# First mixture of experts: stationary down weights, rows turned by VectorE, results gathered by token

## The chip, the cores and the metric

The kernel runs on one core of a Trainium2 chip. A core has TensorE (PE, with its weight loads shown as PEld), VectorE (DVE), ScalarE (ACT), GpSimd (POOL) and SyncE (SP), and 16 DMA engines between its on-chip memory (SBUF, 128 partitions) and DRAM. Products of PE land in PSUM, eight banks of 2 KB per partition. The metric is the device time of one execution in microseconds (us); the median of several runs counts.

## The reference

All data are float32. `x` is a table of 1250 nodes by 1024 features; `src` and `dst` are 20,000 edges.

```python
xn = layernorm(x)
x = x + relu(GCNConv(xn, edges)) + linear_attention0(xn)
x = x + moe0(layernorm(x))                  # 8 experts, top 2, at most 391 rows each
xn = layernorm(x)
x = x + SAGE_two_layers(xn, edges) + linear_attention1(xn)
x = x + moe1(layernorm(x))                  # 8 experts, top 2
```

The change is in `moe0`, the first mixture of experts, and in the norm that follows it:

```python
probs = softmax(x @ router_gate)            # 1250 x 8
topw, topi = top_k(probs, 2); topw /= sum(topw)
top_g, tok_idx = top_k(gates.T, 391)        # the 391 rows with the largest gates, per expert
xe = x[tok_idx]                             # 8 x 391 x 1024
h  = silu(xe @ gate_w) * (xe @ up_w)        # hidden width 512
ye = (h @ down_w) * top_g                   # 8 x 391 x 1024
out = zeros(1250, 1024).at[tok_idx].add(ye)
```

So each expert takes up to 391 rows of 1024, multiplies them by two 1024 x 512 matrices and one 512 x 1024 matrix, and the weighted results are added back to the rows that they came from. A row has at most two results.

## The kernel before, in words

The program is a long sequence of stages, each bounded by PE: gather of the edges into a dense adjacency table, the first norm with projections and attention, the graph convolution, routing, the first experts, the second norm with the second attention, the SAGE layers, and the second experts. The whole network stands twice in the program; the second copy runs only for edge lists that need it (`tc.If(many == 1)`), and not in these runs. Rows lie in 10 tiles of 128 (the last has 98). A tile framework gives each operation to its engine's queue in an order that a scheduler decides; on one engine the instructions run in that order, and a waiting instruction holds up those behind it. DMAs are issued from queues too: SP's for most loads, ACT's for some stores, POOL's for indirect ones (gathers and scatters by an index). Pools hand out buffers: a tile of a pool with `bufs=2` waits until the last but one with its name is no longer used. `wpool` has three buffers of 2 MB for all weights. A float32 matmul is two instructions in the trace.

The stages around the change:

**Routing** (L551 to L734). For each tile the norm `normalise` (L587) writes the rows to a DRAM table `x1n_d`; logits, the two experts of each row with their weights `wts`, and the rank of each row within its expert (`above`, L703) follow. The rows of an expert are put in 392 slots, in 4 groups of `GS` = 98. A product of 0/1 matrices (`at_slot` L714, `hit` L717, `what` L719, the matmul `ptab` L726) makes a table with a token index (`idx`) and a gate for each slot. A slot that stays empty points at a spare row behind the 1250.

**First experts** (L738 to L783). The loop runs over 8 experts. For each: four indirect gathers of 98 rows (`xe`, L744, POOL's queue); 32 transposes on PE (`pte`, L750) that turn the rows to `xeT` (features on partitions), evacuated by ACT and DVE in turns (`evac`, L110 and L112); the loads of `wg`, `wu` (L119) and `wd` (L757) on SP's queue; for each of four blocks of 128 hidden features, 8 matmuls each for gate and up (L764), with the weights stationary and 392 columns of `xeT` moving; the Silu on ACT (L766) and the product `hT` on DVE (L767). The down product (L774) has `hT` stationary, 98 columns of it, and `wd` moving, 512 columns; 4 groups x 2 halves x 4 blocks. DVE (L779) and ACT (L777) multiply by the gate to `ye`, and an indirect DMA (L780) adds the rows to the residual `res_d[1]` in DRAM.

**The second norm and the value product** (L789 to L829). POOL clears `proj` and `kv` (L791, L795); SP loads `proj`, `bqT`, `bkT`, biases and the rows. For each of 10 tiles: load `xt` (L825), statistics and norm in place (`layernorm`, L127: BN statistics L130, aggregate L132, square root on ACT L134, reciprocal L136, norm L137), 8 transposes on PE (L145) evacuated to `x1T` by ACT and DVE, 8 matmuls of 512 columns for the value product `pv` (L152) and an addition of the bias (`v`, L829). The keys `pqT` (L807) follow, then a second half of the value columns with weights of its own.

Of the kernel before, what the change touches and what calls it, by code (L numbers as in the profile page):

```python
# [10 lines left out]
F32 = mybir.dt.float32  # L11
# [3 lines left out]
I32 = mybir.dt.int32  # L15
# [27 lines left out]
GS = 98  # L43
NG = SLOTS // GS
# [10 lines left out]
def tile_gps(ctx: ExitStack, tc: tile.TileContext, a: dict, out: bass.AP):  # L55
# [17 lines left out]
    e.ones = const.tile([P, P], F32, name="ones")  # L73
    nc.vector.memset(e.ones, 1.0)
    e.ones_r = const.tile([P, P], F32R, name="ones_r")
    nc.vector.tensor_copy(e.ones_r, e.ones)
# [5 lines left out]
    e.x1n_d = dram.tile([N + GS, D], F32, name="x1n_d")  # L82
# [3 lines left out]

    e.res_d = [dram.tile([N + GS, D], F32, name=f"res{i}_d") for i in range(4)]

# [8 lines left out]
def network(tc: tile.TileContext, a: dict, out: bass.AP, env: SimpleNamespace, exact: bool):  # L97
# [29 lines left out]
    def layernorm(dst, x, ts):  # L127
        st = small.tile([P, 2, 6], F32, name="st")
        for j in range(2):
            nc.vector.bn_stats(st[:ts, j, :], x[:, j * 512:(j + 1) * 512])  # L130
        mv = small.tile([P, 2], F32, name="mv")
        nc.vector.bn_aggr(mv[:ts], st[:ts].rearrange("p a b -> p (a b)"))  # L132
        sd = small.tile([P, 1], F32, name="sd")
        nc.scalar.activation(sd[:ts], mv[:ts, 1:2], AF.Sqrt, bias=eps_t[:ts])  # L134
        rs = small.tile([P, 1], F32, name="rs")
        nc.vector.reciprocal(rs[:ts], sd[:ts])  # L136
        nc.vector.tensor_scalar(dst, x, mv[:ts, 0:1], rs[:ts], op0=OP.subtract, op1=OP.mult)  # L137
# [414 lines left out]
    idx = rp.tile([GS, E * NG], I32, name="idx")  # L552
    gate = rp.tile([GS, E * NG], F32, name="gate")
    with tc.tile_pool(name="route0a", bufs=1) as ra, tc.tile_pool(name="route0w", bufs=2) as rw:
        zero = ra.tile([GS, P], F32, name="zero")
        nc.gpsimd.memset(zero, 0.0)
        for rows in (x1n_d[N:N + GS, :], env.res_d[1][N:N + GS, :]):
            nc.sync.dma_start(rows.rearrange("p (r c) -> p r c", c=P), zero.unsqueeze(1).to_broadcast([GS, KB, P]))
# [3 lines left out]
        trash = ra.tile([P, 1], F32, name="trash")  # L562
        nc.gpsimd.iota(trash, pattern=[[0, 1]], base=N + 1, channel_multiplier=1, allow_small_or_imprecise_dtypes=True)
        slots = ra.tile([P, GS], F32, name="slots")
        nc.gpsimd.iota(slots, pattern=[[1, GS]], base=0, channel_multiplier=0, allow_small_or_imprecise_dtypes=True)
# [8 lines left out]
        wts = ra.tile([P, T, 2], F32, name="wts")  # L574
# [127 lines left out]

        above = ra.tile([P, T, 2], F32, name="above")  # L703
# [4 lines left out]
        nc.vector.tensor_scalar(grp, above, GS - 0.5, None, op0=OP.is_gt)  # L708
        for j in range(2, NG):
            nc.vector.scalar_tensor_tensor(grp, above, j * GS - 0.5, grp, op0=OP.is_gt, op1=OP.add)  # L710
        nc.vector.scalar_tensor_tensor(above, grp, -float(GS), above, op0=OP.mult, op1=OP.add)
        nc.vector.scalar_tensor_tensor(grp, expert, float(NG), grp, op0=OP.mult, op1=OP.add)
        nc.vector.scalar_tensor_tensor(grp, keep, 1000.0, grp, op0=OP.mult, op1=OP.add)
        at = tb.tile([P, T, 2, GS], F32, name="at_slot")  # L714
        nc.vector.tensor_tensor(at, slots.unsqueeze(1).unsqueeze(1).to_broadcast([P, T, 2, GS]),
                                above.unsqueeze(3).to_broadcast([P, T, 2, GS]), op=OP.is_equal)
# [3 lines left out]
        what = tb.tile([P, T, 2, 2, E * NG], F32, name="what")  # L720
        nc.vector.tensor_mul(what[:, :, :, 0], hit, token.unsqueeze(3).to_broadcast([P, T, 2, E * NG]))
        nc.vector.tensor_mul(what[:, :, :, 1], hit, wts.unsqueeze(3).to_broadcast([P, T, 2, E * NG]))
        pt = bank("ptab")
        for t in range(T):
            for k in range(2):
                nc.tensor.matmul(pt[:GS, :2 * E * NG], at[:TS[t], t, k, :],  # L726
                                 what[:TS[t], t, k].rearrange("p a g -> p (a g)"),
                                 start=(t == 0 and k == 0), stop=(t == T - 1 and k == 1))
        nc.scalar.copy(gate, pt[:GS, E * NG:2 * E * NG])
        row = ra.tile([GS, E * NG], F32, name="row")  # L730
        nc.vector.tensor_scalar(row, pt[:GS, :E * NG], 0.5, trash[:GS], op0=OP.is_lt, op1=OP.mult)
        nc.vector.scalar_tensor_tensor(row, pt[:GS, :E * NG], -1.0, row, op0=OP.add, op1=OP.add)
        nc.vector.tensor_copy(idx, row)
# [3 lines left out]

    with s_route:  # L738
        with tc.tile_pool(name="moe0", bufs=2) as mp:
            for e in range(E):  # L740
                xeT = mp.tile([P, KB, SLOTS], F32, name="xeT")
                for g in range(NG):
                    xe = mp.tile([GS, D], F32, name="xe", bufs=4)
                    nc.gpsimd.indirect_dma_start(  # L744
                        out=xe, out_offset=None, in_=x1n_d,
                        in_offset=bass.IndirectOffsetOnAxis(ap=idx[:, e * NG + g:e * NG + g + 1], axis=0))
                    for b0 in (0, 4):
                        pt = bank("pte")
                        for b in range(4):
                            nc.tensor.transpose(pt[:, b * GS:(b + 1) * GS], xe[:, (b0 + b) * P:(b0 + b + 1) * P],  # L750
                                                ident[:GS, :GS])
                        evac(xeT[:, b0:b0 + 4, g * GS:(g + 1) * GS],
                             pt[:, :4 * GS].rearrange("p (b q) -> p b q", b=4))
                wg = load_w(a["L0_ffn_gate_w"][e], 0, "wg")
                wu = load_w(a["L0_ffn_up_w"][e], 0, "wu")
                wd = wpool.tile([P, I0 // P, D], F32, name="wd", tag="w")
                nc.sync.dma_start(wd, a["L0_ffn_down_w"][e].rearrange("(k p) f -> p k f", p=P))  # L757
                hT = mp.tile([P, I0 // P, SLOTS], F32, name="hT")
                for i in range(I0 // P):
                    ic = slice(i * P, (i + 1) * P)  # L760
                    pg, pu = bank("pgate"), bank("pup")
                    for pw, w in ((pg, wg), (pu, wu)):
                        for k in range(KB):
                            nc.tensor.matmul(pw[:, :SLOTS], w[:, k, ic], xeT[:, k, :], start=(k == 0), stop=(k == KB - 1))  # L764
                    sg = mp.tile([P, SLOTS], F32, name="sg")
                    nc.scalar.activation(sg, pg[:, :SLOTS], AF.Silu)  # L766
                    nc.vector.tensor_mul(hT[:, i, :], sg, pu[:, :SLOTS])  # L767
                for g in range(NG):
                    ye = mp.tile([GS, D], F32, name="ye", bufs=3)
                    own = gate[:, e * NG + g:e * NG + g + 1]  # L770
                    for half in range(2):
                        py = bank("py")
                        for i in range(I0 // P):
                            nc.tensor.matmul(py[:GS], hT[:, i, g * GS:(g + 1) * GS], wd[:, i, half * 512:(half + 1) * 512],  # L774
                                             start=(i == 0), stop=(i == I0 // P - 1))
                        if half:
                            nc.scalar.activation(ye[:, 512:], py[:GS], AF.Copy, scale=own)  # L777
                        else:
                            nc.vector.tensor_scalar(ye[:, :512], py[:GS], own, None, op0=OP.mult)  # L779
                    nc.gpsimd.indirect_dma_start(  # L780
                        out=env.res_d[1], out_offset=bass.IndirectOffsetOnAxis(
                            ap=idx[:, e * NG + g:e * NG + g + 1], axis=0),
                        in_=ye, in_offset=None, compute_op=OP.add)  # L783
# [5 lines left out]
    with tc.tile_pool(name="mix1", bufs=1) as mp:  # L789
# [23 lines left out]
        with tc.tile_pool(name="mix1k", bufs=2) as kp:  # L813
            for half in range(2):
                wv = load_w(a["L1_mix_Wv"], half * 512, "wv1")
                bv = bcast(kp, a["L1_mix_bv"], half * 512, 512, "bv1", bufs=1)
                wk = load_w(a["L1_mix_Wk"], half * 512, "wk1")
                v = kp.tile([P, T, 512], F32, name="v1", bufs=1)
# [3 lines left out]
                for t in range(T):  # L822
                    if half == 0:
                        xt = lnp.tile([P, D], F32, name="xt2")
                        nc.sync.dma_start(xt[:TS[t]], env.res_d[1][TOK[t], :])  # L825
                        layernorm(xt[:TS[t]], xt[:TS[t]], TS[t])
                        transpose_rows(xT, xt[:TS[t]], t, KB)
                    pv = rows_of(xT, t, wv, "pv1")
                    nc.vector.tensor_add(v[:TS[t], t, :], pv[:TS[t]], bv[:TS[t]])  # L829
                s_ln.close()  # L830
                for pair in range(4):
                    hp = half * 4 + pair
                    kT = heads_T(kp, wk, bkT, half, pair)
                    kf = kp.tile([P, T, P], F32, name="kf1")
# [14 lines left out]
                    for j in range(2):  # L849
                        nc.vector.tensor_copy(kv[j * 64:(j + 1) * 64, hp, j * 64:(j + 1) * 64],  # L850
                                              pkv[j * 64:(j + 1) * 64, j * 64:(j + 1) * 64])
        with tc.tile_pool(name="attn1T", bufs=1) as ap_:
# [415 lines left out]
```

## Time and profile before

| what | value |
| --- | --- |
| runs | 3616.58, 3617.64, 3618.37 us; median 3617.64 |
| profiled execution | 3615.68 us; its span, first to last instruction: 3613.9 us |
| mean granted PE clock | 0.971 of full speed |
| PE busy | 3447.9 us (95%), 12658 instructions |
| PEld (weight loads, beside PE) | 2064.1 us (57%) |
| DVE busy | 846.4 us (23%), 2356 instructions |
| ACT busy | 315.8 us (9%) |
| POOL busy | 546.5 us (15%) |
| DMA | 326.25 MB, mean 90 GB/s |
| chain that ended last | PE 90%, DVE 4%, DMA 2%, waiting for issue 2% |

A row of a group names the line, the engine, the operation, output and inputs by the program's names, the shape and the count; then busy time in us and the mean of one in ns, and the idle time before it with what ended it. The mean of one matmul is its latency; matmuls are pipelined, so the time that one adds is a stretch divided by its count. A row of the chain gives start, duration, engine, and what it worked on. A row of the table by stretch gives, for one stretch of time, the busy us (and count) of PE, PEld, DVE, ACT and POOL, the granted clock, the share of DMA and the GB/s moved.

### The profile page before, as it was taken

Reading aid. Unit: us, or ns where it says so; the run is one execution under the profiler, and the core shown is the slowest. Engines: PE = TensorE matmul, PEld = TensorE weight load, DVE = VectorE, ACT = ScalarE, POOL = GpSimd, SP = SyncE. Lnnn points to the kernel's source line nnn. Section 1 sums busy time; section 2 is a strip of 40 time slices with the busy share of each in tenths; the row PEclk is TensorE's granted clock in tenths of the full one; section 3 lists DMA queues with packets and bytes.
Section 4 is the critical chain, followed back from the end, with each engine's and each line's share of the span. In section 5 each row is a group of like instructions: output and inputs, shape, how many; then the busy total and the mean of one; then the engine's idle time right before and its main releaser. Section 6 shows DMA issues by size and latency. Waiting matters only on the chain.

```text
span 3613.9 us, 30826 instructions
## 1 busy us (share of the span) xinstructions
PE 3447.9 (95%) x12658; PEld 2064.1 (57%) x12658; DVE 846.4 (23%) x2356; ACT 315.8 (9%) x640; POOL 546.5 (15%) x442
## 2 busy tenths in 40 slices
PE   7999999999997799999979999999999999988997
PEld 3474756644655554555435465546777555556775
DVE  4256344521226301100130000001111111241111
ACT  1000011100001000100011011100000000001111
POOL 0016774051000011111100000010000000003221
PEclk9999999999997699999989999999999999998999
DMA  4725221162232144544430010131000010228884
GB/s 147 167 69 108 24 24 1 46 223 71 74 105 71 36 132 134 144 117 123 123 97 27 24 47 24 44 103 43 24 24 24 35 58 28 79 81 275 278 257 99
DMA packets 165824, 326.25 MB, mean 90 GB/s; under 512 B 36590, under 2 KB 46261, under 8 KB 165545
## 3 DMA queue, kind: packets, MB, share of 16 engines
q1 hardware_dynamic: 114984, 242.08, 20.1%
q0 software_dynamic: 40016, 54.11, 8.7%
q10 hardware_dynamic: 10672, 27.99, 2.2%
q8 instruction: 102, 1.67, 0.2%
q14 instruction: 50, 0.40, 0.0%
HBM read 250.37 MB, written 73.76 MB: 90 GB/s over the span
## 4 chain that ended last, share of the span: by engine, by line
PE 90%; DVE 4%; DMA 2%; issue 2%; ACT 1%; POOL 0%; SPq 0%; ACTq 0%; POOLq 0%; DVEq 0%
PE ph L152 8%; PE ppn L152 8%; PE pwo L152 8%; PE pv L152 8%; PE pqT L807 7%; PE py L774 6%; PE pqk L152 5%; PE p L1198 5%; PE pa L491 5%; PE pgate L764 5%; PE pup L764 5%; PE ph L929 4%; PE py L1209 2%; PE pg L491 2%; PE pkv L345 2%; PE po L393 2%
## 5 line engine op out<-in xcount | busy, mean ns | idle before, releaser
L253 POOL DMA_INDIRECT adj_d<-cnt,cell x167 | 260.0, 1557 | 92.3 <-issue 42.6
L774 PE MATMUL py<-wd,hT 128*98 128x512 f32 x512 | 221.0, 592 | 0.0
L1198 PE MATMUL p<-xeT,w 128*128 128x256 f32 (+1 forms) x1088 | 192.7, 338 | 5.0 <-ACT xeT L110 5.0
L1198 PEld LDWEIGHTS p<-xeT,w 128*128 128x128 f32 x1088 | 171.3, 191 | 25.1 <-ACT xeT L110 9.0
L764 PE MATMUL pgate<-xeT,wg 128*128 128x392 f32 x512 | 175.9, 497 | 1.7 <-ACT xeT L110 1.7
L764 PE MATMUL pup<-xeT,wu 128*128 128x392 f32 x512 | 173.8, 492 | 0.0
L176 POOL TENSOR_TENSOR xr<-xr,bo 128x512 f32<-128x512 f32 (+1 forms) x40 | 50.4, 1264 | 770.4 <-DMA xr<-res_d 601.4
L774 PEld LDWEIGHTS py<-wd,hT 128*98 128x98 f32 x512 | 84.5, 165 | 133.5 <-issue 132.3
L152 PE MATMUL pqk<-wk,x0T 128*128 128x512 f32 (+1 forms) x320 | 145.2, 608 | 9.0 <-ACT x0T L110 7.6
L152 PE MATMUL pv<-wv,x1T 128*128 128x512 f32 (+1 forms) x320 | 141.8, 601 | 2.2 <-ACT x1T L110 2.2
L152 PE MATMUL ph<-ws,h1T 128*128 128x512 f32 (+1 forms) x320 | 143.2, 596 | 0.0
L152 PE MATMUL pqk<-wq,x0T 128*128 128x512 f32 (+1 forms) x320 | 140.7, 593 | 0.0
L764 PEld LDWEIGHTS pgate<-xeT,wg 128*128 128x128 f32 x512 | 97.3, 191 | 72.9 <-ACT xeT L110 3.2
L152 PE MATMUL ppn<-wn,x1T 128*128 128x256 f32 (+1 forms) x640 | 138.8, 379 | 0.0
L929 PE MATMUL ph<-x1T,ws 128*128 128x416 f32 (+1 forms) x384 | 138.2, 512 | 0.0
L152 PE MATMUL pv<-wv,x0T 128*128 128x512 f32 (+1 forms) x320 | 138.0, 592 | 0.0
L152 PE MATMUL ph<-wgcn,x0T 128*128 128x512 f32 (+1 forms) x320 | 138.0, 593 | 0.0
L764 PEld LDWEIGHTS pup<-xeT,wu 128*128 128x128 f32 x512 | 97.3, 190 | 71.3
L152 PE MATMUL pwo<-wo,attn0T 128*128 128x512 f32 (+1 forms) x320 | 137.7, 592 | 0.2 <-ACT attn0T L410 0.2
L152 PE MATMUL ppn<-wn,h1T 128*128 128x512 f32 (+1 forms) x320 | 137.7, 592 | 0.0
L152 PE MATMUL pwo<-wo,attn1T 128*128 128x512 f32 (+1 forms) x320 | 137.5, 592 | 0.0
L807 PE MATMUL pqT<-x1T,wk 128*128 128x416 f32 (+1 forms) x384 | 135.6, 512 | 0.0
(356 smaller groups left out, 4409.3 us busy)
## 6 DMA issues: line engine op xcount, KB each, us to landing
w<-in_L_ffn_w_dram SPq DMA_DIRECT2D x17, 2048.0 KB
w<-in_L_ffn_w_dram SPq DMA_DIRECT2D x17, 1024.0 KB
wg<-in_L_ffn_gate_w_dram SPq DMA_DIRECT2D x8, 2048.0 KB
wu<-in_L_ffn_up_w_dram SPq DMA_DIRECT2D x8, 2048.0 KB
wd<-in_L_ffn_down_w_dram SPq DMA_DIRECT2D x8, 2048.0 KB
adj_d<-ezero SPq DMA_DIRECT2D x2, 6105.0 KB
res_d<-xr SPq DMA_DIRECT2D x45, 256.0 KB
table<-adj_d ACTq DMA_DIRECT2D x36, 312.5 KB
```

Source lines behind the costliest of these rows:

```text
L152: nc.tensor.matmul(pr[:TS[t], :cols], xT[:, k, TOK[t]], w[:, k, :], start=(k == 0), stop=(k == nk - 1))
L176: nc.gpsimd.tensor_add(xr[:TS[t]], xr[:TS[t]], bias[:TS[t]])
L253: nc.gpsimd.indirect_dma_start(out=adj_d[e % 2], out_offset=bass.IndirectOffsetOnAxis(ap=cell[:, e:e + 1], axis=0), in_=cnt[:, e:e + 1], i ...
L345: nc.tensor.matmul(pkv[f][:, :65], kf[:TS[t], i, f * P:(f + 1) * P], v[:TS[t], t, h, :], start=(t == 0), stop=(t == T - 1))
L393: nc.tensor.matmul(po[:TS[t], i, :], qf[:, hh, f, i * P:i * P + TS[t]], kv[:, h, f, :], start=(f == 0), stop=(f == 1))
L491: nc.tensor.matmul(pa, edges if by_node else feats, feats if by_node else edges, start=(s == 0 and i == 0), stop=(s == T - 1 and i == len( ...
L764: nc.tensor.matmul(pw[:, :SLOTS], w[:, k, ic], xeT[:, k, :], start=(k == 0), stop=(k == KB - 1))
L774: nc.tensor.matmul(py[:GS], hT[:, i, g * GS:(g + 1) * GS], wd[:, i, half * 512:(half + 1) * 512], start=(i == 0), stop=(i == I0 // P - 1))
L807: nc.tensor.matmul(pq[:, :n], w[:, k, pair * P:(pair + 1) * P], xT[:, k, c0:c0 + n], start=(k == 0), stop=(k == KB - 1))
L929: nc.tensor.matmul(ps[:, :n], w[:, k, q0 + f * P:q0 + (f + 1) * P], xT[:, k, c0:c0 + n], start=(k == 0), stop=(k == KB - 1))
L1198: nc.tensor.matmul(pw_[:, :n], w12[:, k, off + i * P:off + (i + 1) * P], xeT[:, k, :n], start=(k == 0), stop=(k == KB - 1))
L1209: nc.tensor.matmul(py, hT[:, i, c * P:(c + 1) * P], w3[:, i, half * 512:(half + 1) * 512], start=(i == 0), stop=(i == H1 // P - 1))
```

## The change

Six things change together.

1. **Down product.** `wd` is stationary: for `b` in 0 to 7 the columns `b`, `b+8`, `b+16`, ... (128 of them, 8 apart), and `hT` moves, 392 columns. The result has features on partitions; DVE turns it in blocks of 32 x 32 to `ye` (slots on partitions), after a clear of the 24 columns by which PSUM's 392 are padded to 416.
2. **Rows turned by DVE.** For experts 1 to 7 POOL gathers quarter rows (1 KB each, 128 of them in one DMA, 13 DMAs an expert) into `xq`, laid so that transposes of 32 x 32 blocks on DVE, four an expert, make `xeT`. The gathers and transposes of expert e + 1 are written in the middle of expert e. The first expert keeps gathers of whole rows, 4 of 128 with two buffers, and transposes on PE. `xeT` holds features in the order p x 8 + k, so `wg` and `wu` are loaded with 8 neighbouring rows in each partition.
3. **Slots.** Groups have 128 slots in place of 98. The table product loses the gates and is float32r in place of float32; a second small product (`pspread`) spreads the index table over quarters (`idx_q`).
4. **Results by token.** Each expert's rows are written, not weighted, to a new DRAM table `y_d` by four DMAs. The scatter-add to the residual goes. In the loop of the second norm each tile gathers its two result rows by `slot_of` (POOL), adds them with the weights `wts` on DVE, and writes the sum to `res_d[1]` from ACT's queue, before the norm overwrites the rows in place.
5. **Order.** The gathers and additions of a tile are issued after the norm of the tile before (`issue_after` sets an order, no wait). The weights of the second half are issued after the last tile's row load. A Sqrt on ACT is placed ahead of the norms.
6. **Small ones.** The ones come from the identity; the spare rows are one each; the key pools move.

```diff
 # routing
-        at = tb.tile([P, T, 2, GS], F32, name="at_slot")
+        at = tb.tile([P, T, 2, P], F32R, name="at_slot")
...
-                nc.tensor.matmul(pt[:GS, :2 * E * NG], at[:TS[t], t, k, :],
-                                 what[:TS[t], t, k].rearrange("p a g -> p (a g)"),
+                nc.tensor.matmul(pt[:, :E * NG], at[:TS[t], t, k, :], what[:TS[t], t, k],
                                  start=(t == 0 and k == 0), stop=(t == T - 1 and k == 1))
-        nc.scalar.copy(gate, pt[:GS, E * NG:2 * E * NG])
...
+        pt = bank("pspread")
+        for i in range(4):
+            nc.tensor.matmul(pt[:, i * E * NG:(i + 1) * E * NG], spread_r[:, i, :], row, start=True, stop=True)
...
+        nc.vector.tensor_copy(idx_q, four)
...
+        nc.vector.tensor_copy(env.slot_of, above)
 # first experts
+            def columns(e):
+                xeT = mp.tile([P, KB, ROWS], F32, name="xeT")
+                if e == 0:
+                    for g in range(NG):
+                        n = min(P, SLOTS - g * P)
+                        xe = mp.tile([P, D], F32, name="xe", bufs=2)
+                        nc.gpsimd.indirect_dma_start(
+                            out=xe, out_offset=None, in_=x1n_d,
+                            in_offset=bass.IndirectOffsetOnAxis(ap=idx[:, g:g + 1], axis=0))
+                        for b0 in (0, 4):
+                            pt = bank("pte")
+                            for b in range(4):
+                                nc.tensor.transpose(pt[:, b * P:b * P + n], xe[:n, b0 + b::KB], ident[:n, :n])
+                            evac(xeT[:, b0:b0 + 4, g * P:g * P + n], pt.rearrange("p (b q) -> p b q", b=4)[:, :, :n])
+                else:
+                    xq = mp.tile([P, NI, B, KB], F32, name="xq")
+                    for i in range(NI):
+                        g = e * NG + i // 4
+                        nc.gpsimd.indirect_dma_start(
+                            out=xq[:, i].rearrange("p c b -> p (c b)"), out_offset=None, in_=quarters,
+                            in_offset=bass.IndirectOffsetOnAxis(ap=idx_q[:, i % 4, g:g + 1], axis=0))
+                    for i0 in range(0, NI, 4):
+                        i1 = min(i0 + 4, NI)
+                        nc.vector.transpose(xeT.rearrange("p b (i r) -> p i b r", r=B)[:, i0:i1],
+                                            xq[:, i0:i1].rearrange("p i c b -> p i b c"))
+                return xeT
...
+                    nc.sync.dma_start(w, a[f"L0_ffn_{name}_w"][e].rearrange("(p k) f -> p k f", k=KB))
...
+                    if i == 1 and e + 1 < E:
+                        coming = columns(e + 1)
+                xeT = coming
+                ye = mp.tile([P, NI, B, KB], F32, name="ye")
+                for b in range(KB):
+                    py = bank("py")
+                    for i in range(I0 // P):
+                        nc.tensor.matmul(py[:, :SLOTS], wd[:, i, b::KB], hT[:, i, :],
+                                         start=(i == 0), stop=(i == I0 // P - 1))
+                    nc.vector.memset(py[:, SLOTS:ROWS], 0.0)
+                    nc.vector.transpose(ye[:, :, :, b], py[:, :ROWS].rearrange("p (i r) -> p i r", r=B))
+                for j in range(4):
+                    (nc.sync if e == E - 1 and j % 2 else nc.scalar).dma_start(
+                        env.y_d[e * ROWS:(e + 1) * ROWS, j * KB * B:(j + 1) * KB * B].rearrange("(i r) f -> r i f", r=B),
+                        ye[j * B:(j + 1) * B].rearrange("p i c b -> p i (c b)"))
+    root = small.tile([P, 1], F32, name="root")
+    tc.keep_in_program_order(nc.scalar.activation(root, eps_t, AF.Sqrt))
 # second norm
+                with ExitStack() as s_after:
+                    if half:
+                        s_after.enter_context(tc.issue_after(last_rows.ins))
+                    wv = load_w(a["L1_mix_Wv"], half * 512, "wv1")
...
-                        nc.sync.dma_start(xt[:TS[t]], env.res_d[1][TOK[t], :])
-                        layernorm(xt[:TS[t]], xt[:TS[t]], TS[t])
-                        transpose_rows(xT, xt[:TS[t]], t, KB)
+                        last_rows = nc.sync.dma_start(xt[:ts], env.res_d[1][TOK[t], :])
+                        s_y = ExitStack()
+                        if t:
+                            s_y.enter_context(tc.issue_after(last_norm.ins))
+                        for k in range(2):
+                            yt = lnp.tile([P, D], F32, name=f"yt{k}", bufs=2)
+                            nc.gpsimd.indirect_dma_start(
+                                out=yt[:ts], out_offset=None, in_=env.y_d,
+                                in_offset=bass.IndirectOffsetOnAxis(ap=env.slot_of[:ts, t, k:k + 1], axis=0))
+                            nc.vector.scalar_tensor_tensor(xt[:ts], yt[:ts], env.wts[:ts, t, k:k + 1], xt[:ts],
+                                                           op0=OP.mult, op1=OP.add)
+                        s_y.close()
+                        nc.scalar.dma_start(env.res_d[1][TOK[t], :], xt[:ts])
+                        last_norm = layernorm(xt[:ts], xt[:ts], ts)
+                        transpose_rows(xT, xt[:ts], t, KB)
```

## The prediction, made before the change was run

> **What bounds the kernel now.** First the page: PE is busy 95% of the span and PE makes 90% of the chain that ended last, so time is gained only where PE's own work shrinks or where PE stands still. Then the chain in order of time (start, us, what), for the stages that the change touches:
>
> ```profile
> 1226.98 6.64 DMA xe<-x1n_d,idx
> 1235.23 6.79 PE pgate L764 x16
> ...
> 1278.89 27.47 PE py L774 x64
> 1309.29 5.53 PE pgate L764 x16
> 1314.83 5.27 PE pup L764 x16
> ...
> 1382.09 5.54 PE pgate L764 x16
> ...
> 1788.50 27.48 PE py L774 x64
> 1817.04 8.89 DMA res_d<-ye,idx
> 1829.99 5.99 DMA xt<-res_d
> 1842.30 8.60 PE pv L152 x16
> ...
> 1924.90 16.79 PE pqT L807 x48
> ```
>
> One expert lasts 1382.09 - 1309.29 = 72.8 us: 8 groups of 5.27 (gate and up, 42.1), 27.47 of the down product, and 3.2 left for the 32 transposes of the next rows and their evacuation. The experts run back to back; the last down product ends at 1815.97, and PE then stands still for 26.3 us, until 1842.30. Ten tiles of norm, transposes and value product follow until 1924.90, 82.6 us, 8.25 a tile (1852.01, 1860.26, 1868.51 in the same chain).
>
> Next the table by stretch, for the expert stage (PE, PEld, DVE, ACT, POOL busy, clock, DMA share, GB/s):
>
> ```profile
> 1235.00:1816.00 581.00, 579.30 (x1762) 298.69 (x1760) 58.49 (x93) 50.77 (x93) 71.70 (x56) 1.00 0.45 123
> ```
>
> PE is full, DVE is a tenth busy, DMA not half: room for work taken off PE. Last, rows that price the new operations, from the groups, the timeline and the DMA view of 108 to 148 us (1.6 KB rows written to DRAM):
>
> ```profile
> L774 PE MATMUL py<-wd,hT 128*98 128x512 f32 x512 | 221.0, 592 | 0.0
> L764 PE MATMUL pup<-xeT,wu 128*128 128x392 f32 x512 | 173.8, 492 | 0.0
> L767 DVE TENSOR_TENSOR hT<-sg,pup 128x392 f32<-128x392 f32 x32 | 18.0, 563 | 324.6 <-PE pup L764 324.6
> L540 DVE SCALAR_TENSOR_TENSOR xrg<-rgcn,xrg 128x512 f32<-128x512 f32 (+1 forms) x10 | 6.9, 692 | 0.3
> ```
> ```profile
> 3305.40 7.22 PEld L1198 LDWEIGHTS p<-xeT,w 128*128 128x128 f32 x64 [0.62 <-ACT xeT L110]
> ```
> ```profile
> DMA packets 5632, 9.01 MB, mean 225 GB/s; under 512 B 32, under 2 KB 5630, under 8 KB 5630
> ```
>
> **1. The down product, weights stationary.** It was 64 instructions a expert (each float32 matmul is two) of 512 columns with 98 of 128 weight columns used: 27.47/64 = 0.429 us each. It becomes 8 x 4 matmuls, again 64 instructions, of 392 columns, as in gate and up: 5.27/16 = 0.329. 64 x 0.329 = 21.1; 6.4 saved, x8 = 51.3 us, all on PE's path.
>
> The weights are now read at every eighth column, 32 bytes apart; no stationary operand before is read so. The Trainium skill, "SBUF — State Buffer", section "Door 1: The DMA port swizzle", speaks against this: a line is 16 bytes, and each access that crosses into a new one "pays a penalty", of no stated size. The row: 64 contiguous loads follow each other in 7.22 us, 0.113 each, under matmuls of 128 columns; the new matmuls last 0.329. By the row alone the loads are covered; by the rule, a load two or two and a half times as long is covered still, and costs begin at 2.9 times. I take nothing, with 0 to +120 us (5 times) as the ends, leaning to 0 because 0.113 leaves almost three loads of room.
>
> **2. The row transposes leave PE.** For experts 1 to 7 the 3.2 us a expert go: 7 x 3.2 = 22.2 us. DVE does them as 3.25 transposes of 1024 elements and 8 of 416 from PSUM. No DVE transpose is in the trace; the nearest rows, 392 elements in 0.563 and 512 in 0.692 (1960 in 2.19, at_slot), give about 1.04 ns an element plus 0.16: 1.22 and 0.59 us. In the built order DVE does the four hT products, two row transposes, a memset, the third, the first ye, the fourth, and then memset and ye in turn. At these prices that is some 11 us within the 21 of the down product. The cover: the next rows are due when it ends. Even at four times the price the row transposes and the first ye take 17 us of 21; no gain is excluded below that, and the ends are 0 and +10. I take 0. The ye copies with the gates (0.75 DVE, 0.69 ACT) go too, off the path.
>
> POOL issues 13 gathers of quarter rows a expert, at 1.28 us pitch (0.97 busy, 0.30 gap, as xe has it): 17 of 63 us, where 8 gathers and scatters were; a whole expert ahead, so nobody waits. The gate weights may load from 5.27 + 21.1 = 26.4 us before they are needed (35.6 before); gate and up together, 4 MB, took 15 us after 1273.65, so they stay hidden. ye is stored by four DMAs on ACT's queue, 1.4 us of issue, done before the next Silu, 5.3 us later.
>
> **3. The first expert.** The table product has half the columns and becomes one float32r instruction each: 20 x 0.173 instead of 6.92, -3.5; one product (0.82) less, at_slot +0.63, small ones +0.36, a copy -0.2: index 3.5 earlier. But xe has two buffers, and in POOL's order five gathers of expert 1 stand before the third xe: third issue at 7 x 1.28 = 9.0 after the first instead of 2.6. The first gather was usable 4.5 us after issue (1223.09 to 1227.62), the next each 1.85 later for 98 rows, 2.4 for 128; third at 13.5, fourth at 15.6, transposes 1.3, evacuation 0.5: 17.4 where 1235.15 - 1223.09 = 12.1 were. +5.4 - 3.5: **+2 us**, ends -2 and +6.
>
> **4. From the last product to the value product**, after 1815.97. Memset and ye 1.1; 1.7 MB to y_d in 1 KB rows at the 225 GB/s of the 1.6 KB rows, 7.6, with 1.2 around it: 9.9. POOL's two memsets (0.95 + 1.09) wait for the pool's memory and stand before the gathers: 12. SP sends bqT, bkT, proj and bv before xt, as before (3 us), so xt goes at 12.7 beside yt0 and yt1; sharing the engines, xt lands at 18, yt1 at 20.5. Two additions of 1.22 (692 for 512): 21.8. The sum is stored before the norm overwrites it in place: norm written at 27.4, transposes on a PE slowed by idling (1.94 before) and evacuation: 30. Before 26.3: **+3.7 us**, ends -2 and +10.
>
> **5. The ten tiles.** New on DVE: two additions, 2.45 us a tile, and the wait of the norm (in place) for the store of the sum. The last x3n_d store (0.4 MB) moved its data from 0.7 to 2.5 us after issue; 0.5 MB alone would be 3.2, beside the next tile's gathers I take 4.6 (ends 3.2 and 8). Statistics, Sqrt and reciprocal (2.2) lie under it. Queued behind that wait on DVE are x1T's copy and the next tile's additions; PE waits for the copy, which the built order puts behind the next norm. A tile on DVE: 2.45 + 0.1 + 4.6 + 0.81 (norm) + 0.68 (copy) = 8.65, about 8.8 with the gaps, where PE needs 8.25. The norm of tile 9 then ends at 27.4 + 9 x 8.8 = 106.6; copy and bias 1.4, half of pv 3.5, transposes and evacuation 1.75, last pv 7.1: 120.3, so 90.3 after pv began, 82.6 before: **+7.7 us**, ends 0 and +27 (11 us a tile). Per tile 2 MB in 8.8 us is 238 GB/s; the late experts moved 281 with DMA 0.92 busy, so it fits, barely. The later weights (half 1) have 170 us until needed: nothing.
>
> Sum: -51.3 - 22.2 + 2 + 3.7 + 7.7 = -60.1 us. The profiled execution took 3615.68 (span 3613.9), 2 us under the median of the runs, 3617.64; the difference is carried over: **3557.5 us**.
>
> **Rivals.** (a) The tiles stay with PE (the store lands within 3.5 us, DVE under 8.25 a tile): part 5 is 0 and part 4 about +1, 3547. For it: DVE was only 31 of 83 us busy there. Against: the DVE chain is serial. 0.17. (b) Transfers bind the tiles: gathers at 217 GB/s, load and store share the engines, 12 us a tile: +36 instead of +7.7, 3586. For it: DMA 0.92 busy at 281. 0.13. (c) Slower: in the down product the strided weight loads outlast the matmuls. It decides from 0.329, and the whole gain is gone at 0.329 + 60/512 = 0.446 us, 3.9 times the row's 0.113; at five times, 0.565, the kernel takes 512 x 0.236 = 121 more, 3678. 0.04. (d) The change doesn't free PE: DVE transposes over five us each make PE wait for the rows, 20 us an expert back, about 3610. 0.02. The forecast itself: 0.64.
>
> **How the numbers follow.** 3543 holds (a) with a few us to spare, 3586 takes in most of (b); outside lie (c), (d) and the rest of (b), under 0.2. Runs of before lie 1.8 us apart; 0.2% (7 us) is about what a measurement of this kernel can tell from no change. Faster 0.95; same 0.02, from (d); slower 0.03, the worse part of (c).
>
> **What would show it.** Expert period 63.2 us, py in 21.1, no pte between experts; PEld on py under 0.33 apart; DVE transposes near 1.2 and 0.6 and all of them over before the next pgate; pv beginning 30 us after the last py; tiles 8.8 apart, with DVE's norm waiting for the DMA of res_d. Wrong if the period is over 66 us, or the tiles are over 11 apart.

## The result, and the profile after

The changed kernel takes 3581.14 us (median of 4 runs, 3578.65 to 3586.95) against 3617.32 (4 runs): a ratio of 0.9902, interval 0.9885 to 0.9919, 36 us less. The forecast was 3557.5, range 3543 to 3586. The sign and the range hold; 24 of the 60 us of gain that were forecast are missing.

First the chain that ended last, in order of time, for the stages that the change touches (start, us, engine and what):

```profile
1229.16 6.30 DMA xe<-x1n_d,idx
...
1236.56 7.84 PE pgate L809 x16
...
1249.67 3.29 PE pgate L809 x10
1252.96 1.44 issue
1254.39 0.49 PE pgate L809
1254.88 1.61 issue
1256.49 0.49 PE pgate L809
1256.98 2.32 issue
...
1303.41 21.07 PE py L821 x64
1324.48 5.27 PE pgate L809 x16
...
1387.68 5.27 PE pgate L809 x16
...
1745.81 21.08 PE py L821 x64
...
1768.55 9.42 DMA y_d<-ye
...
1781.76 9.53 DMA yt<-y_d,slot_of
...
1792.83 5.30 DMA res_d<-xt
...
1826.27 2.69 DMA res_d<-xt
...
1848.13 4.29 DMA res_d<-xt
...
1857.30 7.30 DMA res_d<-xt
...
1889.63 16.79 PE pqT L855 x48
```

The first value product is not in this chain; PE's timeline has it:

```profile
1800.91 8.91 PE L158 MATMUL pv<-wv,x1T 128*128 128x512 f32 x16
```

The expert period is 1387.68 - 1324.48 = 63.2 us, the down product 21.07: both as forecast. But the first expert is not like the others: from its first gate product (1236.56) to its down product (1303.41) go 66.9 us, where 42.1 is PE's own work and the kernel before took 1278.89 - 1235.23 = 43.7. In between the chain is made of pieces of "issue": PE waits for nothing that the profile shows. The text calls this the standstill. The ledger, in us, against the kernel before:

| stretch | before | after | difference | forecast |
| --- | --- | --- | --- | --- |
| up to the first gate product | 1235.23 | 1236.56 | +1.3 | +2 |
| first expert up to its down product | 43.7 | 66.9 | **+23.2** | 0 |
| the rest of the experts, to the last down product | 537.1 | 463.5 | -73.6 | -73.5 |
| last down product to the value product | 26.3 | 34.0 | +7.7 | +3.7 |
| value product to the keys | 82.6 | 88.7 | +6.1 | +7.7 |
| after the keys | | | -0.4 | 0 |

The sum is -35.7, and the profiled executions are 3579.93 and 3615.68, -35.75. The forecast is met to 4 us in each stretch but one.

What the standstill looks like: the table by stretch (stretch, its length; busy us and count of PE, PEld, DVE, ACT, POOL; granted clock, DMA share, GB/s), and the longest waits between 1236 and 1282 (who waited for what: us in total, times, longest us; "remote" and "issue" name no engine):

```profile
1250.00:1278.00 28.00, 10.82 (x20) 4.49 (x20) 0.00 (x0) 0.50 (x1) 17.40 (x19) 0.65 0.30 91
```
```profile
DVE hT L813 <- remote: 35.7, 1, 35.7
ACT sg L812 <- issue: 28.0, 1, 28.0
PEld pgate L809 <- issue: 14.3, 13, 2.6
ACT sg L812 <- remote: 13.0, 1, 13.0
PEld pup L809 <- issue: 11.0, 8, 3.2
```

For 28 us PE does 20 matmuls, DVE nothing and ACT one Silu. Only POOL works, and what it works on are gathers of quarter rows. The DMA engines are 0.30 busy, so they are not full. PE, ACT and DVE are late together, so it is hardly one engine's own wait. Nor did PE wait for instructions to be loaded. The DMA view has no transfer of an instruction queue from 1235 to 1280; the next one (0.02 MB) lies between 1280 and 1285, when PE had already gone on (1276.79).

In the timeline the first Silu starts at 1265.61, though its product was through at about 1244.4, and the first hidden product on DVE at 1279.06, 7 us after POOL's last gather of that row (1271.93). POOL issued 43 gathers one after another, without a pause, from 1219.01 on (below: a row of gathers): four for the first expert, 13 each for the second and third into two buffers, and 13 more once DVE had turned the first buffer (1243).

### The profile page after: what moved, and what is told of

It is laid out like the page before. It is cut to its first block, busy times and chain, and to the rows that moved or that the text cites. A ratio compares the mean times of both kernels' runs of the same rounds, so it can differ in the third digit from the quotient of the medians.

```text
span 3578.2 us, 30558 instructions
## 1 busy us (share of the span) xinstructions
PE 3381.7 (95%) x12418; PEld 2119.7 (59%) x12418; DVE 939.7 (26%) x2482; ACT 281.5 (8%) x580; POOL 581.2 (16%) x493
## 4 chain that ended last, share of the span: by engine, by line
PE 88%; DVE 5%; DMA 4%; issue 2%; ACT 1%; POOL 0%; SPq 0%; ACTq 0%; POOLq 0%; DVEq 0%
PE ph L158 8%; PE ppn L158 8%; PE pwo L158 8%; PE pqT L855 8%; PE pv L158 6%; PE pqk L158 6%; PE p L1265 5%; PE pa L497 5%; PE pgate L809 5%; PE pup L809 5%; PE py L821 5%; PE ph L996 4%; PE py L1276 2%; PE pg L497 2%; PE pkv L351 2%; PE po L399 2%
## 5 line engine op out<-in xcount | busy, mean ns | idle before, releaser
L821 PE MATMUL py<-hT,wd 128*128 128x392 f32 x512 | 169.8, 492 | 0.0
L821 PEld LDWEIGHTS py<-hT,wd 128*128 128x128 f32 x512 | 160.5, 314 | 9.0
```

The source lines that it names most:

```text
L821: nc.tensor.matmul(py[:, :SLOTS], wd[:, i, b::KB], hT[:, i, :], start=(i == 0), stop=(i == I0 // P - 1))
```

## The experiments

All edits are to the changed kernel. "First expert" below is the time from the first gate product to the first down product, read from each run's chain; 42.1 us of it are PE's own work.

**One buffer for the quarter rows.**

```diff
-                    xq = mp.tile([P, NI, B, KB], F32, name="xq")
+                    xq = mp.tile([P, NI, B, KB], F32, name="xq", bufs=1)
```

> One buffer for the quarter rows in place of two, nothing else. In the changed kernel POOL issues 43 gathers without a pause at the start (four for the first expert, 39 for the next three), and PE, ACT and DVE stand nearly still from 30 us into that row of gathers until it ends; the down product of the first expert begins 66.9 us after the first gate product, where 42.1 is PE's own work. Theory 1, the unbroken row of gathers causes the standstill: with one buffer POOL pauses after 17 gathers until DVE has turned them, so the row is broken, the down product begins 42 to 46 us after the first gate product, and the kernel takes 3557 to 3562 us. Theory 2, something else at the first expert causes it (cold PE, its own transposes, DVE's work): still about 67 us, and 3579 to 3585 us.

Measured: 3559.98 us (ratio to before 0.9839, 0.9822 to 0.9855), first expert 44.8. POOL pauses after 17 gathers (4.4 us from the last of them to the next), and the standstill is gone. The stretch from 1250 to 1278 in this kernel:

```profile
1250.00:1278.00 28.00, 28.00 (x86) 16.16 (x86) 1.69 (x3) 0.99 (x2) 9.63 (x11) 1.00 0.18 53
```

**Three buffers.**

```diff
-                    xq = mp.tile([P, NI, B, KB], F32, name="xq")
+                    xq = mp.tile([P, NI, B, KB], F32, name="xq", bufs=3)
...
-                hT, coming = mp.tile([P, I0 // P, SLOTS], F32, name="hT"), None
+                hT, coming = mp.tile([P, I0 // P, SLOTS], F32, name="hT", bufs=1), None
...
-                    sg = mp.tile([P, SLOTS], F32, name="sg")
+                    sg = mp.tile([P, SLOTS], F32, name="sg", bufs=1)
```

> Three buffers for the quarter rows in place of two (to make room, one buffer each for the hidden product and the Silu, which are read before they are written again). The row of gathers at the start grows from 43 to 56, 16 us longer. Theory 1: the standstill begins at the same place and ends with the row, so the down product of the first expert begins 80 to 84 us after the first gate product, and the kernel takes 3594 to 3599 us. Theory 2, a fixed cost at the first expert: 67 us and 3579 to 3585 us as in the changed kernel.

Measured: 3598.39 us (0.9941, 0.9924 to 0.9957), first expert 84.5, half a us above what was expected; the row has 56 gathers and lasts until 1293.09. The loss grows with the row: 17.7 us for 13 gathers more. These two runs leave theory 1 standing and theory 2 not.

**Pauses between the gathers, number and buffers kept.**

```diff
+                        lull = mp.tile([P, 900], F32, name="lull", bufs=1)
+                        nc.gpsimd.memset(lull, 0.0)
```

> After each gather of quarter rows POOL clears a scratch tile (0.9 us), so the gathers are about 2.1 us apart instead of 1.26; their number and the two buffers stay. If it is the rate of the gathers that the other engines cannot keep up with, the standstill is gone: down product 42 to 46 us after the first gate product, 3555 to 3562 us. If it is the number of gathers without a pause between them, the standstill comes after as many gathers, later, and costs about as much: 3575 to 3590 us. A pause of POOL's DMA issue without a change of buffers tells the two apart.

Measured: 3557.87 us (0.9834, 0.9817 to 0.9850), first expert 44.1. The same 43 gathers, 1.99 us apart, cost PE nothing. The same stretch as above, in this kernel:

```profile
1250.00:1278.00 28.00, 28.00 (x87) 16.17 (x86) 3.69 (x4) 1.49 (x3) 25.73 (x29) 1.00 0.29 83
```

PE is busy for all 28 us, with the DMA share as it was (0.29 and 0.30): the share is not what decides.

**A shorter pause** (400 columns cleared in place of 900).

> POOL clears a smaller scratch tile after each gather of quarter rows, about 0.4 us, so that the gathers are some 1.5 us apart (1.26 in the changed kernel with 24 us of standstill, 1.99 in the paced run with none). If a backlog grows with what exceeds a rate near one gather in 2 us, about 9 gathers fill it in 30 us at 1.26 and the same takes 60 us at 1.5, so at most 5 us of standstill are left at the end of the row: down product 42 to 48 us after the first gate product. If any rate well above one in 2 us holds the engines up after a fixed number of gathers, 10 us or more are left.

Measured: 1.57 us apart, first expert 44.9 (one run, 3553.51). No standstill is left, so the limit lies between one gather in 1.57 and one in 1.26 us (128 KB each: between 83 and 104 GB/s).

**Half the rows in each gather.**

```diff
+                    nc.vector.memset(xq[64:].rearrange("p i c b -> p (i c b)"), 0.0)
...
-                            out=xq[:, i].rearrange("p c b -> p (c b)"), out_offset=None, in_=quarters,
-                            in_offset=bass.IndirectOffsetOnAxis(ap=idx_q[:, i % 4, g:g + 1], axis=0))
+                            out=xq[:64, i].rearrange("p c b -> p (c b)"), out_offset=None, in_=quarters,
+                            in_offset=bass.IndirectOffsetOnAxis(ap=idx_q[:64, i % 4, g:g + 1], axis=0))
```

> Each gather of quarter rows fetches 64 rows instead of 128; the other half of the buffer is cleared by DVE, so half of the features of experts 1 to 7 are left out of the computation. As many gathers, at the same or a smaller distance, with half the rows and bytes. If it is the rows (each one a transfer of 1 KB) that the engines are held up by, the standstill is gone or nearly so, down product 42 to 47 us after the first gate product. If it is the gather instructions, it stays: 55 us or more, unless the gathers come so much faster that the row is over before 30 us have passed.

Measured: 43 gathers in the row, 1.22 us apart, first expert 44.4 (one run, 3561.61). So the gather instructions alone, in a row 51 us long, don't do it.

**As many rows, half the bytes.**

```diff
-        quarters = x1n_d.rearrange("n (j f) -> (n j) f", j=4)
+        eighths = x1n_d.rearrange("n (j f) -> (n j) f", j=8)
...
+                    nc.vector.memset(xq[:, :, 16:, :], 0.0)
...
-                            out=xq[:, i].rearrange("p c b -> p (c b)"), out_offset=None, in_=quarters,
+                            out=xq[:, i, :16].rearrange("p c b -> p (c b)"), out_offset=None, in_=eighths,
```

> Each gather fetches 128 rows of 512 bytes instead of 1 KB, from the first half of the table by the same indices; DVE clears the other half of the buffer. Experts 1 to 7 so compute with other rows and half of the features. As many gathers and as many rows as in the changed kernel, at the same distance of 1.26 us, with half the bytes. 64 rows of 1 KB had no standstill. If the number of rows holds the engines up: the standstill stays, down product 62 to 70 us after the first gate product, PE busy 10 to 14 of the 28 us from 1250 to 1278. If the bytes do: none, 42 to 47 us, PE busy all of the 28.

Measured: 43 gathers in the row, 1.26 us apart, first expert 44.1 (one run, 3555.53):

```profile
1250.00:1278.00 28.00, 28.00 (x86) 16.18 (x85) 1.69 (x3) 1.49 (x3) 18.35 (x20) 1.00 0.21 56
```

128 rows in 1.26 us are harmless too when they have 512 bytes. Of the three, gathers, rows and bytes, only the bytes are left as what has to be over a limit. The DMA packets that carry them can't be told from them: both runs halved these too (packets over 512 bytes, 1245 to 1270: 30 a gather in the changed kernel, 16 with 64 rows, 15 with 512-byte rows). And a high rate is not enough: the row must also be long. The later experts' 13 gathers at the same 1.26 us (16 us long, during the down product) hold nobody up.

**Row transposes back on PE**, gathers of whole rows for all experts, two buffers.

```diff
-                if e == 0:
+                if e < E:
...
-                            in_offset=bass.IndirectOffsetOnAxis(ap=idx[:, g:g + 1], axis=0))
+                            in_offset=bass.IndirectOffsetOnAxis(ap=idx[:, e * NG + g:e * NG + g + 1], axis=0))
```

> All experts take the path of the first: gathers of whole rows (four of 128, two buffers) and transposes on PE; the rest as in the changed kernel. The second part of the change is undone: 32 transposes an expert come back on PE, about 3.2 us for each of seven experts, 22 to 25 us in all, if every gather is on time. Theory 1: no row of gathers, no standstill, 23 us less; the two cancel and the kernel takes 3576 to 3586 us, with the down product of the first expert 43 to 47 us after its first gate product. Theory 2: the standstill stays, 3600 to 3608 us.

Measured: 3639.64 us, slower than before (1.0058, 1.0041 to 1.0074), first expert 55.9: both expectations missed. The timeline at the second expert:

```profile
1337.03 1.95 PE L781 MATMUL pte<-ident,xe 128*128 128x128 f32 x16
...
1342.48 1.94 PE L781 MATMUL pte<-ident,xe 128*128 128x128 f32 x8 [3.50 <-DMA xe<-x1n_d,idx]
...
1346.00 8.30 PE L809 MATMUL pgate<-xeT,wg 128*128 128x392 f32 x16
```

PE's transposes stand in the middle of an expert; the third gather can only go out when PE has freed a buffer (1338.36), and PE waits for it. The stop also slows the next group to 8.30 us where 5.27 is usual. So this run prices the two buffers, not the transposes. Once more with four buffers, as the kernel before had them (`name="xe", bufs=4`):

> The run with the row transposes on PE once more, with four buffers for the gathered rows instead of two. With two, the third gather of an expert had to wait for PE's transposes in the middle of the expert before, PE then stood still for 7 us an expert, and that run came out at 3639.6. With four, each gather is issued a whole expert ahead. Then the price of the row transposes on PE is seen alone: 63.2 + 3.2 to 3.6 us a period for seven experts, with no standstill at the first, 3558 + 23 to 25 = 3578 to 3585 us. If the first run's loss was not the buffers, it stays above 3620.

Measured: 3581.19 us (0.9897, 0.9881 to 0.9914), as much as the changed kernel. From the first gate product to the end of the last down product it takes 532.8 us; the run with one buffer for the quarter rows takes 508.2. So DVE's row transposes are worth 24.6 us (forecast 22.2), and the standstill of 23.2 had taken nearly all of that back.

**The norm into a buffer of its own.**

```diff
-                        last_norm = layernorm(xt[:ts], xt[:ts], ts)
-                        transpose_rows(xT, xt[:ts], t, KB)
+                        xn = lnp.tile([P, D], F32, name="xn2", bufs=2)
+                        last_norm = layernorm(xn[:ts], xt[:ts], ts)
+                        transpose_rows(xT, xn[:ts], t, KB)
```

> In the ten tiles the norm writes a buffer of its own (two of them), so DVE no longer waits for the store of the sum; nothing else is changed, the standstill at the first expert stays. Theory 1 (the prediction's): the wait for the store bounds the tiles. Then the first norm comes 3.5 us earlier, and the tiles fall back to PE's 8.25 each: from the last down product to the keys 116 to 119 us instead of 122.8, and 3574 to 3579 us in all. Theory 2: the transfers bound them (2 MB a tile at 202 GB/s mean): the first norm comes earlier, but the tiles stretch by as much, 121 to 124 us, and 3579 to 3584 us.

Measured: 3573.99 us (0.9878, 0.9862 to 0.9895). Its chain, at two of the tiles and the keys:

```profile
1810.95 7.13 PE pv L158 x16
...
1819.19 7.13 PE pv L158 x16
...
1883.83 16.79 PE pqT L855 x48
```

The value products follow each other at 8.24 us, PE's own pace; the store is in the chain no more. From the last down product (1771.43) to the keys are 112.4 us against 122.7: 10.3 less, more than theory 1 expected, and theory 2 (transfers) has fallen. (This run's first expert took 68.9 us, 2 more than the changed kernel's, so the whole shows only 7.)

**The later weights after the last store.**

```diff
-                        s_after.enter_context(tc.issue_after(last_rows.ins))
-                    wv = load_w(a["L1_mix_Wv"], half * 512, "wv1")
+                        s_after.enter_context(tc.issue_after(last_store.ins))
+                    wv = load_w(a["L1_mix_Wv"], half * 512, "wv1", queue=nc.scalar if half else None)
...
-                        nc.scalar.dma_start(env.res_d[1][TOK[t], :], xt[:ts])
+                        last_store = nc.scalar.dma_start(env.res_d[1][TOK[t], :], xt[:ts])
```

> The weights of the second half of the values are issued from ACT's queue after the last store of a sum, instead of from SP's queue after the last row load; nothing else is changed. In the changed kernel this 2 MB load starts at 1853.6, and the stores of tiles 7 and 8 take 4.3 and 7.3 us instead of 2.7, with norms 9.2 and 11.8 us apart. Theory 1, the load takes the engines from the stores: these two fall to 7.3 to 8.3, the keys come 3 to 6 us earlier, 3575 to 3579 us. Theory 2, the stores are slow there for another reason (last gathers): no change, 3579 to 3584 us.

Measured: 3581.24 us (0.9896, 0.9879 to 0.9912), which decides nothing: the first expert took 69.4 us in this run, 2.6 more. In the stage itself it is 118.6 us from the last down product to the keys instead of 122.7, and from the third value product on the chain runs on PE. The 4 us are what theory 1 expected of the stage, but of its two stores only one became short. From the store's issue to the norm that waits for it, tile 8 (counted from 0) takes 3.1 us where the changed kernel takes 7.4; tile 7 takes 5.5 where it took 4.7. In the changed kernel tile 7's store had landed at 1852.42, before the load was issued at 1853.63, so the load can't have slowed it.

**The strided weight loads alone.** The down product moves 128 columns; experts 0, 2, 4, 6 load contiguous columns.

```diff
-                        nc.tensor.matmul(py[:, :SLOTS], wd[:, i, b::KB], hT[:, i, :],
+                        nc.tensor.matmul(py[:, :P], wd[:, i, b::KB] if e % 2 else wd[:, i, b * P:(b + 1) * P], hT[:, i, :P],
...
-                    nc.vector.memset(py[:, SLOTS:ROWS], 0.0)
+                    nc.vector.memset(py[:, P:ROWS], 0.0)
```

> The strided weight loads by themselves: the down product moves 128 columns of the hidden product instead of 392, and experts 0, 2, 4, 6 take their down weights in contiguous columns, experts 1, 3, 5, 7 at every eighth column as in the changed kernel. Two thirds of the slots and, for the even experts, the order of the features are left out of the computation. If a strided load costs what a contiguous one does (0.113), both kinds take about 7.3 us for 64 instructions, or 8 to 9 where DVE's copies are waited for. If lines of 16 bytes are paid for (the load rows of the changed kernel read 0.314 on average beside 0.191), odd experts take 11 to 20 us, 0.17 to 0.31 each; even ones stay at 7 to 9.

The chain, an even and an odd expert (one run, 3507.93):

```profile
1309.98 7.25 PE py L821 x64
...
1359.37 15.12 PE py L821 x64
```

7.25/64 = 0.113 us a load contiguous, 15.12/64 = 0.236 strided: a strided load costs twice as much.

**Together**: one buffer for the quarter rows, four for the first expert's rows, the norm apart, the weights later.

> What the runs so far point to, together: one buffer for the quarter rows; four buffers for the first expert's rows, so that its four gathers go first on POOL's queue; the norm into a buffer of its own; the later weights from ACT's queue after the last store. From the changed kernel's 3581: 21 less without the standstill (as with one buffer alone), 10.3 less from the last down product to the keys (as with the norm apart), 2 to 4 less before the first gate product (last gather issued at 3.8 instead of 10.2 us after the first, landing some 2.4 us apart), nothing more for the later weights, since PE sets the pace of the tiles: 3546 us, 3542 to 3552. If the gains don't add (a standstill comes back, or the tiles are bound by transfers), 3555 or more.

Measured: 3540.77 us (5 runs, 3538.05 to 3541.95), a ratio of 0.9788 to before (0.9775 to 0.9802), twice the gain of the change and 1 us better than the range expected. First expert 42.3; 113.5 us from the last down product to the keys; the first gate product 11.0 us after the first gather's issue, where the changed kernel needs 17.5: 6.5 less, where 2 to 4 were expected.

## Why the prediction was right and wrong

The measured time lies in the range, but not for a reason that the prediction gave. Its upper end, 3586, was set for tiles bound by transfers (rival (b)); the 24 us were lost in the first expert's gate and up products, where it had put nothing. That the range was wide enough is luck.

**Down product: right.** 64 x 0.329 = 21.07 as measured, 51.3 us. The Trainium skill's rule that lines of 16 bytes are paid for ("SBUF — State Buffer", section "Door 1: The DMA port swizzle") does agree with the chip here: strided loads cost 0.236 us instead of 0.113, 2.1 times. "I take nothing" came out right because 0.236 is still under 0.329, with 1.4 loads of room instead of the "almost three loads" that the text leaned on. By an estimate from these two numbers, a product that moves fewer than 392 x 0.236/0.329 = 281 columns would have lost time by the stride.

**Row transposes: the gain right, a step missing.** The period fell to 63.2. DVE's prices were too low: the nearest rows gave 1.22 and 0.59 us, and the transposes took 2.02 and 0.94 (the groups by line and shape, in the expert stage; mean in ns):

```profile
L824 DVE STREAM_TRANSPOSE ye<-py 128x416 f32<-128x416 f32 x63 | 58.9, 936 | 2.1
L792 DVE STREAM_TRANSPOSE xeT<-xq 128x1024 f32<-128x1024 f32 x20 | 39.7, 2018 | 1.0 <-DMA xq<-x1n_d,idx_q 1.0
```

The cover, reckoned up to four times the price, held it. What failed is the sentence "a whole expert ahead, so nobody waits". It counted the gathers of one expert against one expert's time, and looked only at who waits for their data. At the start nothing holds POOL back: the buffers let three experts' gathers run as one row behind the first expert's four, and that row slowed engines that wait for none of it. This one step is 23.2 of the 24 us. None of the rivals had it. The rate was to be had beforehand: 128 KB each 1.26 us is 104 GB/s; that such a rate does harm was not shown by the trace of before, where gathers came at most eight at a time.

**First expert's index and rows: right.** From the first gather's issue to the first gate product 12.1 became 17.5 us, +5.4 as reckoned; the index was 4.1 earlier (3.5 forecast). The kernel before had four buffers for these rows. The run with all edits, which has four again, shows that the two buffers and the five gathers in between cost it.

**Last product to value product: +7.7 instead of +3.7.** The stores to `y_d` were through at 1778.0, 11.1 after the last product (9.9 forecast), and the first gather went out at 13.6 (12). The larger part is the landing: the sum counted the first tile's three transfers, but POOL issued four gathers and SP three row loads within 4 us, 3.5 MB instead of 1.5, and the first tile's last row table was there 24.4 us after the product (20.5 forecast). From the sum to the written norm, store included, it then took 6.4 us (5.6 forecast), and from there to the value product 1.9 (2.6).

**Tiles: +6.1 instead of +7.7, with other parts.** That the norm waits for the store is shown: the run with the norm apart takes the stage to PE's pace, and in the changed kernel the first norm stands behind it:

```profile
1798.23 0.81 DVE L143 TENSOR_SCALAR xt<-xt,mv,rs 128x1024 f32<-128x1024 f32 x1 [3.46 <-DMA res_d<-xt]
```

The first nine norms are 8.3 us apart on average, not 8.8: the stores take 2.7 us in the middle rather than 4.6, but 5.0 to 5.7 at some of the first tiles and 7.3 at tile 8. There "The later weights (half 1) have 170 us until needed: nothing" failed: their 2 MB are issued at 1853.6, just before that store, and norms 7 and 8 are 11.8 us apart, the only gap beyond the 11 that the prediction named as a sign of being wrong. Rival (a) is what the run with the norm apart makes of the kernel; rival (b), transfers as the bound, has fallen.

## What to carry to other kernels

A load that is early enough need not be free: look at what its queue does when nothing holds it back, above all at the first turn of a loop, when all buffers are empty. Depth of buffers is then a throttle as much as a cover; here one buffer less was 21 us faster. Where a store and the next in-place step share a buffer, a second buffer removes the wait, and a load with time to spare should be queued behind the transfers that have none (4 us in that stage here).

## What the runs showed of the hardware

A row of indirect gathers of 128 rows of 1 KB, 1.26 us apart (104 GB/s), let PE, ACT and DVE fall behind together, from some 33 us after its start until 5 to 6 us after its end. The first expert then took 66.9, 68.9, 69.4 and 70.0 us in four kernels with 43 gathers, 84.5 with 56, where 42.1 are PE's own work. At 1.57 us apart (83 GB/s), with 64 rows (54 GB/s) or with 512 bytes a row (52 GB/s) it did not happen; the last two also halved the packets. Direct loads moved 281 GB/s in the last experts of the kernel before, with PE busy for 34.38 of 35 us, so it isn't DMA bandwidth as such:

```profile
3355.00:3390.00 35.00, 34.38 (x178) 26.34 (x177) 5.74 (x10) 4.92 (x10) 8.54 (x7) 1.00 0.92 281
```

Which path fills up, and why the first Silu starts 21 us after its product is through, no view of the profile shows; it stays open. Whether the recording of the profile takes part can't be told either, since the span and the clock of every execution here come from a recording.
